# Conv-sequence block on one Trainium2 core: softmax laid out by key with no maximum where the weights bound the scores, groups emitted as a pipeline of five steps, one pool of PSUM banks

## The chip, the cores and the metric

The kernel runs on one core of one Trainium2 chip. The core's engines work side by side, each in its own queue's order: TensorE (PE, matrix products into the eight banks of PSUM), VectorE (DVE), ScalarE (ACT, functions such as the exponential), GpSimd (POOL), and SyncE (SP), which issues most DMA transfers. The metric is the device time of one execution in microseconds (us).

## The reference

Input x is [2, 256, 128, 128]: batch, time, band, channel. Three residual steps: attention over time (causal, 4 heads of 32 channels, one sequence of 256 steps for each batch and band), attention over bands (128 bands of one time step, only pairs at most 16 apart), and a feed-forward of 512 with gelu. Each begins with a layer norm over the channels. All data is float32.

```python
def _mha(x, wi, bi, wo, bo, h, mask):
    qkv = x @ wi.T + bi
    ...
    scores = jnp.einsum('...hqd,...hkd->...hqk', q, k) * (1.0 / np.sqrt(dh)) + mask
    attn = jax.nn.softmax(scores, axis=-1)
    o = jnp.einsum('...hqk,...hkd->...hqd', attn, v)
    ...
    return o @ wo.T + bo
...
xt = _ln(x, ln_t_w, ln_t_b).transpose(0, 2, 1, 3)
x = x + _mha(xt, t_wi, t_bi, t_wo, t_bo, H_T, cm).transpose(0, 2, 1, 3)
xf = _ln(x, ln_f_w, ln_f_b)
x = x + _mha(xf, f_wi, f_bi, f_wo, f_bo, H_F, bm)
xn = _ln(x, ln_n_w, ln_n_b)
h = jax.nn.gelu(xn @ w1.T + b1, approximate=False)
x = x + (h @ w2.T + b2)
```

The weight matrices are drawn with a standard deviation of 0.02; the norms' weights are ones, all biases zeros.

## The kernel before

Work goes in groups of four token tiles of 128 rows (NT = 4). In the first stage a group is two sequences of 256 steps; eight bands (four groups) are loaded at once by two DMAs (L278), and the result of each group is stored to a scratch tensor in memory (L287). There are 128 such groups. In the second stage a block is 16 time steps (L299): four groups of attention over bands, then the same four groups through the feed-forward, then the store (L332). There are 32 blocks.

Every group is written from start to end before the next, by `norm_transposed` (L113) and `attention` (L134). In order: statistics of the rows (L118, L119 on DVE), their inverse deviation (rstd, L121 and L122 on POOL), the normalized rows (xh, L126 on DVE), transposes on PE (L129) and a scaled copy by ACT (xnT, L131); the products for queries, keys and values (L144, L148, L153) with copies by ACT and DVE. The scores stand with queries on the partitions and keys along the row. For each pair of heads a score tile of two banks is filled by a product of the identity with a bfloat16 mask (L166), to which the scores are added (L173, 32 rows of the array for each head). DVE takes the negated maximum of each row (nmax, L181 for bands, L187 for time), ACT the exponential with that shift, 128 or 256 columns at a time, and each row's sum through its accumulator (p and rsum, L195), DVE the reciprocal (L203), POOL the division (L206 for bands, L214 for time). p is then transposed on PE block by block (tp, L221) and copied to SBUF by DVE and ACT in turn (pT, L226, L228). The weighed values (op, L239) come out transposed, are copied with the value bias (oT, L245), multiplied by the output weights (yp, L248), and added to the rows (L249).

A scheduler of the framework orders the instructions of each engine; it follows the order in which the program wrote them, and moves forward what its model finds ready. Score tiles have their own pool of two tiles with two banks each, and every other PSUM tile shares a pool of four banks (L57, L58). Exponentials and gelus need different function tables on ACT; `order_act` (L255) makes them take turns by the block.

## Time and profile before

| | us |
|---|---|
| median of three runs | 6695.87 (6692.37 to 6696.81) |
| span of the profiled execution | 6687.7 |
| PE busy | 4965.1 |
| ACT busy | 3223.4 |
| DVE busy | 2769.3 |
| POOL busy | 2263.4 |

The runs were timed without the profiler, the span comes from the profiled execution, from its first to its last instruction. "Busy" is the time in which at least one instruction of the engine was under way; PE's products are pipelined and overlap. One float32 product appears as two records of PE, the two passes over its moving operand; its weight loads are listed apart as PEld. In a group's row the shapes stand as partitions x elements, then the count, the total and the mean of one in ns, and after the bar the idle time of the engine just ahead and what ended it. A row of the timeline has start, length, engine, line, operation, tiles, shape and the count of records that were merged.

### The profile page before, as it was taken

To read this page: it belongs to the slowest core of one execution; us is meant where nothing else is said; L and a number is where in the kernel's file an instruction comes from. 1 tells how busy PE (TensorE), PEld (TensorE's weight loads), DVE (VectorE), ACT (ScalarE), POOL (GpSimd) and SP (SyncE) were. 2 spreads that over 40 slices of the span, in tenths; PEclk is the share of its full clock that TensorE was granted. 3 is DMA by queue.
4 is the path that set the end of the run, shared out by engine and by line. 5 is a ranking of instruction groups with operands and counts; after the bars stand their busy time and mean duration, and the time that the engine had idled before them with its cause. 6 is when DMAs were issued, how large, how long until landed. Compare 5 with 4: busy or idle time off the path is not lost. (4 is left out here: it accounts for less than half of the span.)

```text
span 6687.7 us, 95401 instructions
## 1 busy us (share of the span) xinstructions
PE 4965.1 (74%) x34688; PEld 3392.3 (51%) x34816; DVE 2769.3 (41%) x8068; ACT 3223.4 (48%) x10688; POOL 2263.4 (34%) x2348
## 2 busy tenths in 40 slices
PE   6777777777777777777777777777676767677767
PEld 4444454444444444454555555555454545455555
DVE  4444444444444444434344444444344444444433
ACT  4444444444444444444454444444444444454544
POOL 4333333333333333433232323233333333233332
PEclk8878787778787877788888888888888888888888
DMA  1000000000000000000000000000000000000000
GB/s 48 20 24 25 23 20 24 24 23 20 24 24 23 20 24 23 24 20 20 24 15 24 14 26 14 26 13 26 13 26 13 26 13 26 13 26 13 20 7 13
DMA packets 222968, 141.61 MB, mean 21 GB/s; under 512 B 7968, under 2 KB 205984, under 8 KB 222496
## 3 DMA queue, kind: packets, MB, share of 16 engines
q1 hardware_dynamic: 221248, 134.45, 7.1%
q8 instruction: 274, 4.49, 0.3%
q14 instruction: 198, 1.62, 0.1%
q10 hardware_dynamic: 1248, 1.05, 0.1%
HBM read 68.36 MB, written 67.11 MB: 20 GB/s over the span
## 5 line engine op out<-in xcount | busy, mean ns | idle before, releaser
L195 ACT ACTIVATE p<-sp,nmax 128x128 f32<-128x128 f32 (+1 forms) x4096 | 1547.6, 414 | 870.0 <-DVE nmax L187 553.6
L221 PE MATMUL tp<-ident,p 128*128 128x128 f32 x5120 | 1207.6, 401 | 275.6 <-POOL p L206 228.0
L221 PEld LDWEIGHTS tp<-ident,p 128*128 128x128 f32 x5120 | 930.1, 209 | 743.0 <-POOL p L206 394.6
L214 POOL TENSOR_TENSOR p<-p,rsum 128x256 f32<-128x256 f32 (+1 forms) x1024 | 823.9, 826 | 952.2 <-DVE rsum L203 820.9
L206 POOL TENSOR_TENSOR p<-p,rsum 128x1024 f32<-128x1024 f32 x256 | 485.2, 1895 | 1493.5 <-DVE rsum L203 1493.5
L195 ACT ACTIVATION_READ_ACCUMULATOR p<-sp,nmax 128x1 f32 x4096 | 929.0, 227 | 0.0
L228 ACT COPY pT<-tp 128x384 f32<-128x384 f32 (+1 forms) x768 | 395.1, 518 | 945.8 <-PE tp L221 942.5
L226 DVE COPY pT<-tp 128x384 f32<-128x384 f32 (+1 forms) x768 | 453.8, 598 | 698.9 <-PE tp L221 689.3
L173 PE MATMUL sp<-kT,qT 32*128 32x128 f32 (+1 forms) x8192 | 740.7, 362 | 0.0
L166 PEld LDWEIGHTS <-ident_b 128*128 128x128 bf16 x1536 | 193.8, 128 | 1007.0 <-issue 663.8
L166 PE MATMUL sp<-mask_t,ident_b 128*128 128x384 bf16 x1024 | 383.1, 472 | 384.6 <-ACT p L195 381.7
L203 DVE RECIPROCAL rsum<-rsum 128x4 f32<-128x4 f32 (+1 forms) x768 | 141.9, 185 | 1221.9 <-ACT p L195 1204.0
L239 PE MATMUL op<-pT,v 128*32 128x128 f32 (+1 forms) x8192 | 526.6, 319 | 86.6 <-DVE pT L226 55.0
L166 PE MATMUL sp<-mask_f,ident_b 128*128 128x512 bf16 x384 | 204.3, 601 | 517.0 <-ACT p L195 517.0
L173 PEld LDWEIGHTS sp<-kT,qT 32*128 32x128 f32 x8192 | 490.8, 214 | 172.9 <-issue 142.1
L317 ACT ACTIVATE hT<-hp,cols_sb 128x512 f32<-128x512 f32 x512 | 351.8, 687 | 392.3 <-PE hp L316 389.5
L187 DVE TENSOR_REDUCE nmax<-sp 128x2 f32<-128x256 f32 (+1 forms) x1024 | 505.0, 545 | 56.6 <-PE sp L173 56.5
L131 ACT ACTIVATE xnT<-xp,cols_sb 128x512 f32<-128x512 f32 x384 | 298.4, 777 | 475.0 <-PE xp L129 475.0
L327 PEld LDWEIGHTS zp<-w2T_sb,hT 128*128 128x128 f32 x4096 | 487.5, 192 | 61.5 <-issue 58.4
L316 PE MATMUL hp<-xnT,w1T_sb 128*128 128x512 f32 x1024 | 471.9, 599 | 42.8 <-ACT xnT L131 27.8
L327 PE MATMUL zp<-w2T_sb,hT 128*128 128x128 f32 x4096 | 499.0, 275 | 0.1
L121 POOL TENSOR_SCALAR rstd<-mv 128x4 f32<-128x4 f32 x384 | 91.8, 242 | 1190.5 <-DVE mv L119 1190.5
(55 smaller groups left out, 5974.5 us busy)
## 6 DMA issues: line engine op xcount, KB each, us to landing
xt<-in_x SPq DMA_DIRECT2D x64, 512.0 KB, 5.5
x<-rd SPq DMA_DIRECT2D x256, 128.0 KB, 1.9
out<-res SPq DMA_DIRECT2D x128, 256.0 KB, 2.3
xb<-x SPq DMA_DIRECT2D x32, 0.5 KB, 6.2
w1T_sb<-in_w1T ACTq DMA_DIRECT2D x1, 256.0 KB, 5.4
w2T_sb<-in_w2T ACTq DMA_DIRECT2D x1, 256.0 KB, 7.1
t_wiT_sb<-in_t_wiT ACTq DMA_DIRECT2D x1, 192.0 KB, 2.5
f_wiT_sb<-in_f_wiT ACTq DMA_DIRECT2D x1, 192.0 KB, 4.5
```

What stands on the lines that cost most here:

```text
L166: nc.tensor.matmul(sp[:, j, 0 : nb * P], ident_b, mask.rearrange("p a b -> p (a b)"), start=True, stop=False,)
L173: nc.tensor.matmul(sp[:, j, n * P : (n + len(ks)) * P], qT[r, qi * P : (qi + 1) * P], kT[r, ks[0] * P : (ks[-1] + 1) * P], start=False, st ...
L187: nc.vector.tensor_reduce(nmax[:, :, ri : ri + 1], sp[:, :, n * P : (n + len(ks)) * P], AX.X, ALU.max, negate=True,)
L195: e = nc.scalar.activation(p[:, j, n * P : (n + len(ks)) * P], sp[:, j, n * P : (n + len(ks)) * P], AF.Exp, bias=nmax[:, j, ri : ri + 1], ...
L206: nc.gpsimd.tensor_tensor(pv, pv, rsum.rearrange("p j n -> p (j n)").unsqueeze(2).to_broadcast([P, 2 * nb, P]), ALU.mult,)
L214: nc.gpsimd.tensor_tensor(pv, pv, rsum[:, :, ri : ri + 1].to_broadcast([P, 2, len(ks) * P]), ALU.mult,)
L221: nc.tensor.transpose(tp[:, n * P : (n + 1) * P], p[:, j, n * P : (n + 1) * P], ident)
L226: nc.vector.tensor_copy(t, tp[:, 0 : nb * P])
L228: nc.scalar.copy(t, tp[:, 0 : nb * P])
L239: nc.tensor.matmul(op[r, qi * P : (qi + m) * P], v[:, ki, r], pT[bi, h][:, n * P : (n + m) * P], start=first, stop=last,)
L316: nc.tensor.matmul(hp_, w1T_sb[:, j * P : (j + 1) * P], xnT, start=True, stop=True)
L327: nc.tensor.matmul(zp[:, i], hT[:, j, i * P : (i + 1) * P], w2T_sb[:, j, :], start=(j == 0), stop=(j == NI - 1),)
```

## The change

The program now begins with `fold` (L334), which multiplies the norms' weights and the score scale into the projection weights, turns the norms' biases into the query bias, the output rows and the feed-forward's bias, and computes a test: with the Gram matrices of a head's query and key weights, the sum of their elementwise product is compared with a bound, and the value and output weights are compared with another. The result goes to a register of every engine, and a branch takes one of two paths: `shifted_path` is the former kernel in full, `bounded_path` the new one.

In `bounded_path` the scores are laid out with keys on the partitions and queries along the row: K is the stationary and Q the moving operand. There is no mask product, no maximum, no transpose of p. ACT takes the exponential of a whole head at once (384 columns over time, 512 over bands), and POOL then sets the masked weights to zero by affine selects, two for each sequence (four heads, 512 elements each) or two for each pair of heads over bands (1024 elements each). The weighed values are a product with p itself (op); a second product, of ones with p, gives each query's sum on all 32 channels of the head (rp). ACT computes Exp(−Ln(rp)), DVE one step of Newton's method on it and the product with op (`divide`: t, u, oT), with the sign turned around in the negated output weights wn. The copies of xnT and of the keys are now DVE's.

A group is an object with steps, and `run` writes the steps of neighbouring groups in turn: in round n stand the transposes of group n + 1, the division of n − 1, the first half of the scores of n, queries and keys of n + 1, the second half of n, the normalizing of n + 2, the output of n − 1, the values of n + 1, the statistics of n + 3, and the weighing of n; loads are written five groups ahead. All PSUM tiles take one bank each from a pool of eight. The table for Exp and Ln is loaded once by name where attention follows a feed-forward.

```diff
-    ps_s = ctx.enter_context(tc.tile_pool(name="ps_s", bufs=2, space=PSUM))
-    ps = ctx.enter_context(tc.tile_pool(name="ps", bufs=4, space=PSUM))
+        self.ps = ctx.enter_context(tc.tile_pool(name="ps", bufs=8, space=PSUM))
...
+def fold(tc, k):
...
+            wf = const.tile([P, 3 * C], F32, name=f"wf{a}")
+            nc.vector.tensor_scalar(wf[:, 0:C], wi[:, 0:C], col(c0), scale, ALU.mult, ALU.mult)
+            nc.vector.tensor_scalar(wf[:, C : 3 * C], wi[:, C : 3 * C], col(c0), None, ALU.mult)
...
+            nc.tensor.matmul(gq, wf[:, 0:C], wf[:, 0:C], start=True, stop=False)
...
+            nc.tensor.matmul(gk, wf[:, C : 2 * C], wf[:, C : 2 * C], start=True, stop=True)
...
+            nc.vector.tensor_tensor(gs, gk, gs, ALU.mult)
...
+                nc.vector.tensor_reduce(tests[r, 3 * a : 3 * a + 1], gs[r, r], AX.X, ALU.add)
...
+                ok[:, 3 * a : 3 * a + 1], tp[:, 3 * a : 3 * a + 1], SAFE * SAFE / (C * (C + 1)), None, ALU.is_le
...
+    return nc.values_load(flag[0:1, 0:1], min_val=0, max_val=1)
...
+    def invert(self):
...
+        path.exp_set(nc.scalar.activation(ln, self.rp, AF.Ln))
...
+        path.exp_set(nc.scalar.activation(self.r0, ln, AF.Exp, scale=-1.0))
...
+    def divide(self):
...
+        nc.vector.tensor_tensor(t, self.rp, self.r0, ALU.mult)
...
+        nc.vector.tensor_tensor(u, self.op, self.r0, ALU.mult)
...
+        nc.vector.scalar_tensor_tensor(self.oT, t, 2.0, u, ALU.subtract, ALU.mult)
...
+class OverTime(Attention):
...
+        for h in range(H):
+            r = rows_of(h)
+            sp = path.bank([P, W], "sp")
+            nc.tensor.matmul(
+                sp[:, 0 : 2 * P], self.kT[r, a : a + P], self.qT[r, a : a + 2 * P], start=True, stop=True
+            )
+            nc.tensor.matmul(
+                sp[:, 2 * P : W], self.kT[r, a + P : a + 2 * P], self.qT[r, a + P : a + 2 * P],
+                start=True, stop=True,
+            )
+            path.exp_set(nc.scalar.activation(self.p[:, s, h, :], sp, AF.Exp))
+        for n in (0, 2):
+            blk = self.p[:, s, :, n * P : (n + 1) * P]
+            nc.gpsimd.affine_select(
+                out=blk, in_=blk, compare_op=ALU.is_ge, fill=0.0, base=0,
+                pattern=[[0, H], [1, P]], channel_multiplier=-1,
+            )
...
+class OverBands(Attention):
...
+        for s in (1, -1):
+            nc.gpsimd.affine_select(
+                out=blk, in_=blk, compare_op=ALU.is_ge, fill=0.0, base=BAND,
+                pattern=[[0, len(heads)], [0, NT], [-s, P]], channel_multiplier=s,
+            )
...
+        for n in range(-5, len(groups) + 1):
...
+            do(n + 5, "load")
+            do(n + 1, "transpose", "bias")
+            do(n - 1, "divide")
+            do(n, "first_half")
+            do(n + 1, "queries_keys")
+            do(n, "second_half")
+            do(n + 2, "normalize")
+            do(n - 1, "output")
+            do(n + 1, "values")
+            do(n + 3, "statistics")
+            do(n, "weigh")
...
+    bounded = fold(tc, k)
+    with tc.If(bounded > 0) as cmp:
+        bounded_path(tc, k, x, out)
+    with cmp.Else():
+        shifted_path(tc, k, x, out)
```

What stands in PE's queue in the middle of the first stage, before the change, from the weighing of one group to the scores of the next (the number behind a tile's name counts tiles, so that tiles of one group lie close together):

```order
L239 MATMUL op_3972<-pT_3970,v_3846 32x128
L248 MATMUL yp_3991<-t_woT_sb_85,oT_3989 128x128 x4
L129 MATMUL xp_4018<-ident_93,xh_4017 128x128 x4
L144 MATMUL qp_4029<-xnT_4027,t_wiT_sb_81 128x512
L148 MATMUL kp_4033<-xnT_4027,t_wiT_sb_81 128x512
L153 MATMUL vp_4037<-t_wiT_sb_81,xnT_4027 128x128 x4
L173 MATMUL sp_4044<-kT_4035,qT_4031 128x128 x2
L173 MATMUL sp_4044<-kT_4035,qT_4031 128x256 x2
```

And PE's queue in the first stage of the changed program, from the last scores of one round to the first scores of the next:

```order
L582 MATMUL sp_3438<-qT_3297,kT_3301 128x128
L550 MATMUL yp_3449<-wn0_106,oT_3397 128x128 x4
L524 MATMUL vp_3457<-wf0_103,xnT_3389 128x128 x4
L608 MATMUL op_3477<-pt_3399,v_3339 32x256 x4
L613 MATMUL op_3477<-pt_3399,v_3339 32x128 x4
L608 MATMUL op_3477<-pt_3399,v_3339 32x256 x4
L620 MATMUL rp_3494<-pt_3399,ones_87 32x512 x4
L613 MATMUL op_3477<-pt_3399,v_3339 32x128 x4
L622 MATMUL rp_3494<-pt_3399,ones_87 32x2x128 x4
L467 MATMUL xp_3507<-ident_76,xh_3444 128x128 x4
L579 MATMUL sp_3523<-qT_3420,kT_3424 128x256
L582 MATMUL sp_3523<-qT_3420,kT_3424 128x128
```

The output of one group, the values of a second and the transposes of a third now stand between the scores and the weighing of a fourth and the next scores; a head's two score products stand side by side, where two heads used to alternate (x2).

DVE's queue in the first stage before, where the statistics of a new load stand:

```order
L249 TENSOR_TENSOR rd<-yp,rd 128x512
L126 TENSOR_SCALAR xh<-xt,mv,rstd 128x128 x4
L119 BN_AGGR mv<-stats 128x2 x4
L157 COPY v<-vp 128x512
L187 TENSOR_REDUCE nmax<-sp 128x2 x4
L118 BN_STATS stats<-xt 128x6 x8
L203 RECIPROCAL rsum<-rsum 128x4
L118 BN_STATS stats<-xt 128x6 x8
```

DVE's queue in the changed program at such a place, once in four groups:

```order
L457 TENSOR_SCALAR xh<-xt,mv,rstd 128x128 x4
L540 TENSOR_TENSOR t<-rp,r_4867 128x512
L542 TENSOR_TENSOR u<-op,r_4867 128x512
L448 BN_AGGR mv<-stats 128x2 x4
L446 BN_STATS stats<-xt 128x6 x8
L544 SCALAR_TENSOR_TENSOR oT<-t,u 128x512
L446 BN_STATS stats<-xt 128x6 x8
L517 COPY kT<-kp 128x512
```

The statistics of four groups, sixteen instructions, stand ahead of and behind the oT that the output product reads; they used to stand among the maxima and reciprocals.

PE's queue in the attention over bands of the changed program, one round:

```order
L642 MATMUL sp_27112<-qT_27020,kT_27024 128x128 x4
L642 MATMUL sp_27118<-qT_27020,kT_27024 128x128 x4
L510 MATMUL qp_27126<-xnT_27102,wf1_143 128x512
L515 MATMUL kp_27130<-xnT_27102,wf1_143 128x512
L667 MATMUL op_27071<-pf_27003,v_26948 32x128 x14
L670 MATMUL rp_27088<-pf_27003,ones_87 32x512 x2
L642 MATMUL sp_27134<-qT_27020,kT_27024 128x128 x4
L642 MATMUL sp_27140<-qT_27020,kT_27024 128x128 x4
```

Here the scheduler put most of the weighing of a group (op, the fifth row, which reads the selected pf of heads 2 and 3 among others) behind the next group's first scores and the queries and keys of the one after; in other rounds it stands ahead of them.

More of the change, by code (lines that the diff above doesn't have):

```diff
@@ L11 @@
 BF16 = mybir.dt.bfloat16
+I32 = mybir.dt.int32
 AF = mybir.ActivationFunctionType
@@ new lines, with bias, hidden, first_half @@
+class FeedForward(Group):
+    def bias(self):
+        path = self.path
+        self.res = path.work.tile([P, NT, P], F32, name="res")
+        path.nc.gpsimd.tensor_tensor(
+            self.res, self.src(), path.k.rows[:, 2:3, :].to_broadcast([P, NT, P]), ALU.add
+        )
+    def hidden(self, js):
+        path, nc = self.path, self.path.nc
+        for j in js:
+            hp = path.bank([P, NT * P], "hp")
+            nc.tensor.matmul(hp, path.k.w1f[:, j * P : (j + 1) * P], self.xnT, start=True, stop=True)
+            path.gelu_set(
+                nc.scalar.activation(
+                    self.hT[:, j, :], hp, AF.Gelu, bias=path.k.b1[:, j : j + 1], scale=1.0
+                )
+            )
+    def first_half(self):
+        self.hT = self.path.work.tile([P, self.path.k.NI, NT * P], F32, name="hT", bufs=2)
+        self.hidden((0, 1))
+    def second_half(self):
+        self.hidden((2, 3))
+    def output(self):
+        path, nc = self.path, self.path.nc
+        NI = path.k.NI
+        zp = path.bank([P, NT, P], "zp")
+        for i in range(NT):
+            for j in range(NI):
+                nc.tensor.matmul(
+                    zp[:, i], self.hT[:, j, i * P : (i + 1) * P], path.k.w2T[:, j, :],
+                    start=(j == 0), stop=(j == NI - 1),
+                )
+        nc.vector.tensor_tensor(self.res, zp, self.res, ALU.add)
+        self.store(self.res)
@@ L29, in conv_seq_kernel, with bounded_path @@
+def bounded_path(tc, k, x, out):
+    with ExitStack() as ctx:
+        BoundedPath(ctx, tc, k).run(x, out)
 @with_exitstack
```

840 lines of the change are left out of this document (589 added, 251 removed).

## The prediction

> **What bounds the kernel now.** I read the engines' shares on the page first, then equal stretches of the two stages, then the chain that ended last, then single groups by shape.
>
> ```profile
> span 6687.7 us, 95401 instructions
> PE 4965.1 (74%) x34688; PEld 3392.3 (51%) x34816; DVE 2769.3 (41%) x8068; ACT 3223.4 (48%) x10688; POOL 2263.4 (34%) x2348
> ...
> 21.60:2844.00 2822.40, 2180.09 (x14160) 1392.00 (x14160) 1200.61 (x3578) 1335.32 (x4720) 1063.83 (x1306) 0.80 0.08 23
> 2890.00:6650.00 3760.00, 2714.27 (x20096) 1951.71 (x20222) 1531.47 (x4344) 1848.04 (x5865) 1166.71 (x992) 0.87 0.07 19
> ...
> 6546.00:6570.00 24.00, 24.00 (x143) 17.78 (x143) 6.11 (x16) 10.58 (x15) 3.08 (x4) 1.00 0.11 33
> 6576.00:6640.00 64.00, 38.32 (x321) 27.50 (x323) 23.30 (x61) 32.08 (x133) 19.01 (x16) 0.82 0.00 1
> ```
>
> No engine is full. In the last two rows (columns: stretch, its length, busy us of PE, PEld, DVE, ACT, POOL, granted clock, DMA) the feed-forward has PE busy all 24 us at clock 1.00; attention over bands has it busy 38 of 64 us at 0.82, and each other engine half or less. The DMA share is under a tenth. So the feed-forward is bound by PE, attention by something that no engine's sum shows. The chain shows it (start, us, what):
>
> ```profile
> 6482.31 1.24 DVE nmax L181
> 6483.63 1.08 ACT p L195 x6
> 6484.93 1.62 ACT p L195 x9
> 6486.91 1.90 POOL p L206
> 6488.86 1.97 PE tp L221 x8
> ...
> 6493.55 0.59 ACT pT L228
> 6494.19 1.07 PE op L239 x26
> 6495.29 0.70 ACT oT L245
> 6496.03 1.16 PE yp L248 x8
> ...
> 6502.51 1.24 DVE nmax L181
> ...
> 6546.89 3.44 PE hp L316 x8
> 6551.21 3.13 PE zp L327 x28
> 6554.33 3.44 PE hp L316 x8
> ```
>
> One group of bands, maximum to maximum, takes 6502.51 − 6482.31 = 20.20 us, and its own steps fill it in single file: maximum, exponentials, division, transposes, weighing, output. **Attention is bound by the latency of one group**, since groups stand one behind another in every queue. A feed-forward group takes 6554.33 − 6546.89 = 7.44 us, PE alone. Over time the first and the last group's query product stand at
>
> ```profile
> 21.61 2.07 PE L144 MATMUL qp<-xnT,t_wiT_sb 128*128 128x512 f32 x2 [0.87 <-ACT xnT L131]
> 2844.02 1.12 PE L144 MATMUL qp<-xnT,t_wiT_sb 128*128 128x512 f32 x2 [0.87 <-ACT xnT L131]
> ```
>
> so 127 periods take 2822.4 us, 22.2 each. From 2866 to the end 32 blocks (four groups of bands, four feed-forwards) take 3822 us, 119.4 each: 4 × 20.2 + 4 × 7.44 = 110.6, and 9 at the changes.
>
> **The change part by part.** The durations it needs:
>
> ```profile
> 1507.89 0.95 PE L173 MATMUL sp<-kT,qT 32*128 32x128 f32 x16
> 1520.83 1.27 PE L239 MATMUL op<-pT,v 128*32 128x256 f32 x20
> 6593.35 1.72 PE L173 MATMUL sp<-kT,qT 32*128 32x128 f32 x32
> ...
> L317 ACT ACTIVATE hT<-hp,cols_sb 128x512 f32<-128x512 f32 x512 | 351.8, 687 | 392.3 <-PE hp L316 389.5
> L228 ACT COPY pT<-tp 128x384 f32<-128x384 f32 x512 | 245.4, 484 | 477.6 <-PE tp L221 474.3 <-PE op L239 1.7
> L317 ACT ACT_TABLE_LOAD x32 | 41.1, 1283 | 0.6
> L214 POOL TENSOR_TENSOR p<-p,rsum 128x512 f32<-128x512 f32 x512 | 531.9, 1039 | 0.0
> L206 POOL TENSOR_TENSOR p<-p,rsum 128x1024 f32<-128x1024 f32 x256 | 485.2, 1895 | 1493.5 <-DVE rsum L203 1493.5
> L97 POOL TENSOR_SCALAR_AFFINE_SELECT mask_f<-mask_f 128x512 bf16<-128x512 bf16 x2 | 1.3, 634 | 0.1
> L90 POOL TENSOR_SCALAR_AFFINE_SELECT mask_t<-mask_t 128x128 bf16<-128x128 bf16 x2 | 0.5, 292 | 0.0
> L282 POOL TENSOR_TENSOR rd<-xt,rows_sb 128x512 f32<-128x512 f32 x128 | 162.2, 1268 | 45.1 <-DMA x<-rd 36.5 <-DMA xt<-in_x 8.5
> L122 POOL TENSOR_TENSOR rstd<-rstd,mhalf 128x4 f32<-128x4 f32 x384 | 399.7, 1047 | 26.1
> L126 DVE TENSOR_SCALAR xh<-xb,mv,rstd 128x128 f32<-128x128 f32 x512 | 271.4, 593 | 297.4 <-PE xp L129 225.2 <-issue 64.8 <-POOL res L321 7.4
> L126 DVE TENSOR_SCALAR xh<-xt,mv,rstd 128x128 f32<-128x128 f32 x512 | 141.5, 339 | 0.0
> L118 DVE BATCH_NORM_STATS2 stats<-xt 128x6 f32<-128x128 f32 x512 | 105.8, 278 | 70.6 <-DMA xt<-in_x 70.2
> L249 DVE TENSOR_TENSOR rd<-yp,rd 128x512 f32<-128x512 f32 x128 | 88.5, 691 | 391.9 <-PE yp L248 391.9
> ```
>
> *Removed*, all on the chain: mask products, maxima (DVE), reciprocals, the division on POOL, transposes of p with their copies. *Added*: selects that zero masked weights (POOL), sums by a product with ones (rp), Ln and Exp on ACT for 1/sum, three DVE passes (t, u, oT). Copies of xnT and kT go from ACT to DVE, folded weights replace their scales.
>
> *PE work of a group* (records are passes, two to a product). Queries and keys: the chain's 3.44 us for eight passes of 512 columns gives 1.72. Values and output: 3.13/28 a pass, eight passes, 0.89 each. Transposes: 0.5. Scores over time: the first row is one sequence's four heads, 0.95 when heads alternate; now a head's two products stand together. Strictly one after another a head holds its 32 rows for (2 × 256 + 2 × 128) columns at 0.43 per 512: 0.55 after the previous head, 2.3 for four. In file, even with alternating heads, each product holds off the next by its first pass: 4 × 0.11 + 4 × 0.22 = 1.3 for the first row's sequence, and 16 × 0.11 + 0.27 of drain = 2.0 for the third row's bands. The rows are 0.95 and 1.72: products on other rows overtake. I take 1.2, nearer the row than to 2.3. So 2.4 for two sequences. Weighing: 1.27 for 20 passes, 32 make 1.6 with one drain. Sums: 2 × (512 + 256) columns with four heads side by side, 1.3 to 1.5. Sum over time: 0.5 + 1.72 + 2 × 0.89 + 2.4 + 1.6 + 1.5 = **9.5 us**. Bands: scores 2.2 (bounds 1.7 and 3.2), weighing 1.3, sums 1.3: **8.8 us**. Feed-forward: unchanged, 7.44.
>
> The Trainium skill ("TensorE: Matmul & The Clock Gate", Part 3: Packing small matmuls — row/col tiling) says that products are strict FIFO in start and end. By that rule the scores of two sequences cost 4.6 instead of 2.4; the 0.95 row does not agree, but it shows alternating heads, not heads in a row, so the rule is rival B.
>
> *The wait that ends last now, over time.* Let 0 be the end of a group's sums. ACT: Ln and Exp, 0.69 each and a hand-over, 1.6, and behind them in its queue stands all that follows of the next group; four exponentials of 384 columns at 0.49, 3.6; query copy, 4.2; four more, 6.3. POOL then selects twice. A select costs 0.178 + 0.00089 per column (292 and 634 ns rows): 0.63 for 512, and 1.04 if it ran like the L214 row; so 7.7 to 8.5. DVE: xnT to 1.5, four xh 2.6, t and u 4.0, aggregates 4.4, oT 5.1. PE: transposes 0.5, scores 1.7, wait for xnT, queries and keys 3.6, scores 4.8, wait for oT 5.2, output and values 7.0, weighing and sums 10.1. The selects end under that. So **PE with its two short waits sets the period**. DVE and POOL can block each other: xh took 339 ns alone and 593 on average where L301 ran beside it; oT meets the first selects, up to 0.6, so 10.1 to 10.7, I take 10.4. One group in four has eight statistics (0.22 apart) ahead of oT: 1.8/4 = 0.45. Period **10.8 us**, where 22.2 was.
>
> *Bands.* The selects are 1024 columns, 1.09 each (1.9 if like L206), two after the last exponential, and weighing needs them: Ln, Exp 1.7; two exponentials of 512 (0.69 each, 0.6 apart, an estimate between the 484 and 687 rows) 3.0; query copy 3.6; scores of heads 2 and 3 at 4.8; exponentials 6.1; selects with hand-overs 8.6; the rest of weighing and sums 10.4. PE waits near 1.5 us of it. **10.5 us**, where 20.2 was. POOL's sum, 4 × 1.09 + 1.27 + 1.29, is 6.9, and DVE's 7 × 0.69 (xnT, kT, v, t, u, oT, output) + 1.1 + 0.9 + 0.4 = 7.2: neither binds.
>
> *Feed-forward and changes.* 7.44 stays. At a change PE goes on with the neighbour's products; I leave 3 us a block for table loads (1.28 each, two) and for the run of 16 statistics before the second feed-forward, where 9 stood. Block: 4 × 10.5 + 4 × 7.44 + 3 = 74.8.
>
> *Queues.* SP now holds each load five groups ahead, behind stores:
>
> ```profile
> xt<-in_x SPq DMA_DIRECT2D x64, 512.0 KB, 5.5
> xb<-x SPq DMA_DIRECT2D x32, 0.5 KB, 6.2
> ```
>
> Landing in 5.5 and 6.2 us lies under five groups of ten: nothing. POOL's additions (1.27) stand ahead of the selects, under the exponentials; ahead of a block's first select four of them stand, under the feed-forward, or 5 us a block if they came late.
>
> *Bank pool.* Eight banks instead of 4 + 2 × 2 cost nothing: each one's earlier reader has ended on the count above; a missed one shows as PE waiting on ACT.
>
> *Start.* fold adds some 45 DVE instructions in a chain with small products, a flag read by all engines, and only then are the first inputs loaded; three groups fill the pipeline. The first query product stood at 21.6; I take 60, bounds 35 and 110. The branch itself is in no row: 0 to some us.
>
> *Clock.* It was 0.80 to 0.82 where PE had gaps and 1.00 where it had none; with gaps of 0.5 to 1.5 us I count 1.0.
>
> Sum: 128 × 10.8 + 32 × 74.8 + 60 = 1382 + 2394 + 60 = 3836. The runs' median of 6695.87 lies 8 above the profile's span; with it **3845 us**.
>
> **Rivals.**
> - A, all waits hidden, PE alone: 128 × 9.5 + 32 × (4 × 8.8 + 29.8) + 60 = 3356, with the 8, 3365. For it: the feed-forward shows PE dense. Against: the bands' loop of 10.4.
> - B, heads in single file: 2.2 more over time, 1.0 more in the bands' loop: 128 × 3.2 = 410, 4255. For it, the order (a head's products together); against, the 0.95 and 1.72 rows.
> - C, selects at the price of L206 and L214: bands' loop +1.6, over time +0.5: 128 × 2.1 = 269, 4115. For it, both work on float32 p in place; against, the rows of selects themselves.
> - D, the clock stays at 0.8: over time PE work 9.5/0.8 = 11.9 swallows the waits, 12.4 with the statistics, +1.6; bands' PE share of the loop, 2.9 us, +0.7: 128 × 2.3 = 294, 4140. For it, row-group products fill a quarter of the array; against, gaps too short.
> - E, slower than before: the test fails and the shifted path runs, the kernel of before with 35 us of fold in front: 6731. It decides at 30²/(128 × 129) = 0.0545 for the sum, over heads, of the products of the query and key Gram matrices. With weights of deviation 0.02, the query's divided by √32, the diagonals give 128 × 0.0016 × 0.0512 = 0.0105. Five times under.
>
> **How the numbers follow.** Forecast 0.48, A 0.11, B 0.17, C 0.12, D 0.10, E 0.02. The prediction is 3845; the forecast's own range is 3600 to 4050. Reaching over B, C and D with some of them together, and to just above A: 3420 to 4400. A measurement can tell 0.2% from no change; only E is not faster: 0.975 faster, 0.005 within, 0.02 slower.
>
> **What would show it.** Period of the query product over time near 10.8, with PE busy over 85% and clock above 0.95 (D: 0.8). Last record of a sequence's scores 1.2 us after the first (B: 2.3). Select rows of 634 and 1090 ns (C: 1040 and 1900). In bands, PE's longest wait on POOL selects, a block near 75 us. Table loads still 64. First query product near 45. The prediction is wrong if DVE or POOL, blocking each other, exceed 10 us a group, or if bank waits tie groups together again.

## The result and the profile after

The changed kernel takes 4108.43 us (median of four runs, 4102.52 to 4109.43); the kernel before, timed beside it, 6696.34. The ratio is 0.6134, interval 0.6125 to 0.6143. The profiled execution has a span of 4106.3 us and took 4108.16, so 2 us lie around it. A later run of the kernel before shows the same (6693.05 with a span of 6691.3); so the 8 us that the prediction added seem to be mostly a difference between executions. The head of the page:

```profile
span 4106.3 us, 77158 instructions
PE 3682.2 (90%) x31270; PEld 2508.3 (61%) x31270; DVE 2327.0 (57%) x6702; ACT 1595.4 (39%) x2880; POOL 1909.9 (47%) x2182
```

Three stretches of the trace (length, busy us of PE, PEld, DVE, ACT and POOL, granted clock, DMA share), from the first to the 128th query product over time, the 30 blocks from the second on, and a short one that is spoken of below:

```profile
36.53:1412.44 1375.91, 1224.49 (x13129) 802.36 (x13129) 848.98 (x2375) 640.40 (x1387) 672.89 (x888) 0.94 0.18 50
1503.19:4006.41 2503.22, 2276.90 (x16802) 1580.81 (x16801) 1367.04 (x3963) 886.86 (x1381) 1152.13 (x1197) 0.96 0.09 25
836.00:844.50 8.50, 7.48 (x64) 5.33 (x64) 4.50 (x13) 0.00 (x0) 1.70 (x2) 0.60 0.12 33
```

A group over time takes 1375.91/127 = **10.83 us** (predicted 10.8), a block 2503.22/30 = **83.4** (predicted 74.8). Times 32, the block is 276 us too long, a little more than the 263 by which the time was missed; the start, earlier than forecast, gives some back. In the first two stretches PE is idle for a tenth and its clock is under 1, so neither is dense.

*Over time.* The 10.83 is no common period: three of four groups take 9.25 us, every fourth 14 to 17. PE's timeline over one short and one long group:

```profile
821.30 1.13 PE L510 MATMUL qp<-xnT,wf 128*128 128x512 f32 x2
...
830.55 1.12 PE L510 MATMUL qp<-xnT,wf 128*128 128x512 f32 x2
...
832.46 0.73 PE L579 MATMUL sp<-qT,kT 32*128 32x256 f32 x8
833.00 0.42 PE L582 MATMUL sp<-qT,kT 32*128 32x128 f32 x8
837.02 2.08 PE L550 MATMUL yp<-wn,oT 128*128 128x128 f32 x8 [3.60 <-DVE oT L544]
838.89 1.92 PE L524 MATMUL vp<-wf,xnT 128*128 128x128 f32 x8
...
846.09 1.13 PE L510 MATMUL qp<-xnT,wf 128*128 128x512 f32 x2
```

830.55 − 821.30 = 9.25, with PE dense; 846.09 − 830.55 = 15.54. Of the 6.3 more, 3.60 is the wait for oT, and the rest half clock behind it: yp takes 2.08 us, which takes 1.16 at full clock (at 2117.88); over the stretch from 836 to 844.5 the granted clock is 0.60. What oT waited for, in the timelines of DVE, SP and POOL:

```profile
832.00 0.68 DVE L542 TENSOR_TENSOR u<-op,r 128x512 f32<-128x512 f32 x1
832.60 0.37 DVE L448 BATCH_NORM_AGGREGATE mv<-stats 128x2 f32<-128x6 f32 x4
834.47 1.65 DVE L446 BATCH_NORM_STATS2 stats<-xt 128x6 f32<-128x128 f32 x8 [1.50 <-DMA xt<-in_x]
836.03 0.94 DVE L544 SCALAR_TENSOR_TENSOR oT<-t,u 128x512 f32<-128x512 f32 x1
...
830.14 1.00 SPq L766 DMA_DIRECT2D xt<-in_x  x2
...
828.85 1.27 POOL L498 TENSOR_TENSOR rd<-xt,orow 128x512 f32<-128x512 f32 x1 [1.50 <-DMA x<-rd]
```

t and u were done at 832.7, yet oT stands behind eight statistics of the load, and the load was issued at 830.14, when POOL's addition (828.85 + 1.27) had read the oldest input buffer for the last time. The addition had itself waited for a store. Nothing needed these statistics yet: counted in DVE's records, statistics run 12 to 14 groups ahead of the next group to be divided, where the program's order has 3.

*Over bands.* PE's and then ACT's and DVE's timeline of one block:

```profile
2126.09 1.03 PE L670 MATMUL rp<-pf,ones 128*32 128x512 f32 x4
2127.05 1.71 PE L642 MATMUL sp<-qT,kT 32*128 32x128 f32 x16
2131.25 2.05 PE L550 MATMUL yp<-wn,oT 128*128 128x128 f32 x8 [2.49 <-DVE oT L544]
...
2140.11 2.27 PE L642 MATMUL sp<-qT,kT 32*128 32x128 f32 x28
2144.37 2.04 PE L550 MATMUL yp<-wn,oT 128*128 128x128 f32 x8 [1.99 <-DVE oT L544]
...
2154.41 1.03 PE L670 MATMUL rp<-pf,ones 128*32 128x512 f32 x4
2158.94 1.13 PE L550 MATMUL yp<-wn,oT 128*128 128x128 f32 x8 [3.50 <-DVE oT L544]
...
2127.17 0.60 ACT L532 ACTIVATE ln<-rp 128x512 f32<-128x512 f32 x1 [2.04 <-PE rp L670]
2127.80 0.63 ACT L534 ACTIVATE r<-ln 128x512 f32<-128x512 f32 x1
2128.46 0.69 DVE L540 TENSOR_TENSOR t<-rp,r 128x512 f32<-128x512 f32 x1 [1.47 <-ACT r L534]
2129.07 0.68 DVE L542 TENSOR_TENSOR u<-op,r 128x512 f32<-128x512 f32 x1
2129.79 1.32 DVE L544 SCALAR_TENSOR_TENSOR oT<-t,u 128x512 f32<-128x512 f32 x1
```

From the end of the sums (2127.12) to the output product it is 4.1 us of Ln, Exp, t, u, oT (4.2 and 3.5 at the two later places); what stood between them in PE's queue was 1.7 or 2.3 us of scores, or nothing. Three such waits make 8 us in this block, 7 on average. PE waited 201 us for oT and 17 for selects in the stretch from 1600 to 4000, where the prediction had the selects as its longest wait:

```profile
PE yp L550 <- DVE oT L544: 201.1, 87, 3.5
PE op L667 <- POOL pf L648: 17.0, 19, 0.9
```

(Columns: who waited for whom, us in total, times, longest.) The groups by shape, with the mean of one in ns:

```profile
L648 POOL TENSOR_SCALAR_AFFINE_SELECT pf<-pf 128x1024 f32<-128x1024 f32 x512 | 595.8, 1167 | 889.8 <-ACT pf L644 875.7
L589 POOL TENSOR_SCALAR_AFFINE_SELECT pt<-pt 128x512 f32<-128x512 f32 x512 | 350.8, 705 | 301.4 <-ACT pt L586 301.2
```

Selects of 1167 and 705 ns stand against 1090 and 634 predicted. The first query product starts at 36.5, where 45 was named and 60 counted with the filling of the pipeline.

### The profile page after: what moved, and what is told of

It is laid out like the page before. It is cut to its first block, busy times and chain, and to the rows that moved or that the text cites. A ratio compares the mean times of both kernels' runs of the same rounds, so it can differ in the third digit from the quotient of the medians.

```text
span 4106.3 us, 77158 instructions
## 1 busy us (share of the span) xinstructions
PE 3682.2 (90%) x31270; PEld 2508.3 (61%) x31270; DVE 2327.0 (57%) x6702; ACT 1595.4 (39%) x2880; POOL 1909.9 (47%) x2182
## 4 chain that ended last, share of the span: by engine, by line
PE 56%; DVE 5%; ACT 3%; POOL 1%; issue 1%; ACTq 0%; POOLq 0%; DVEq 0%
PE zp L709 11%; PE hp L689 11%; PE sp L642 7%; PE rp L670 6%; PE op L667 4%; PE xp L467 4%; PE yp L550 4%; PE vp L524 3%; PE qp L510 3%; PE kp L515 3%; DVE oT L544 2%; DVE t L540 1%; POOL pf L648 1%; DVE u L542 1%; ACT r L534 1%; ACT ln L532 1%
## 5 line engine op out<-in xcount | busy, mean ns | idle before, releaser
L648 POOL TENSOR_SCALAR_AFFINE_SELECT pf<-pf 128x1024 f32<-128x1024 f32 x512 | 595.8, 1167 | 889.8 <-ACT pf L644 875.7
L550 PE MATMUL yp<-wn,oT 128*128 128x128 f32 x2048 | 333.1, 312 | 357.4 <-DVE oT L544 357.4
L691 ACT ACTIVATE hT<-hp,b 128x512 f32<-128x512 f32 x512 | 341.4, 687 | 386.0 <-PE hp L689 382.0
L589 POOL TENSOR_SCALAR_AFFINE_SELECT pt<-pt 128x512 f32<-128x512 f32 x512 | 350.8, 705 | 301.4 <-ACT pt L586 301.2
L689 PE MATMUL hp<-xnT,w1f 128*128 128x512 f32 x1024 | 485.3, 605 | 0.0
L586 ACT ACTIVATE pt<-sp 128x384 f32<-128x384 f32 x1024 | 420.1, 495 | 127.2 <-PE sp L582 126.8
L642 PEld LDWEIGHTS sp<-qT,kT 32*128 32x128 f32 x4096 | 375.3, 186 | 107.6 <-issue 43.9
L642 PE MATMUL sp<-qT,kT 32*128 32x128 f32 x4096 | 420.4, 283 | 0.0
L451 POOL TENSOR_TENSOR rstd<-rstd,mhalf 128x4 f32<-128x4 f32 x384 | 403.8, 1057 | 23.6
L524 PE MATMUL vp<-wf,xnT 128*128 128x128 f32 x2048 | 312.9, 304 | 0.0
```

Source lines behind the costliest of these rows:

```text
L451: nc.gpsimd.tensor_tensor(self.rstd, self.rstd, path.k.mhalf, ALU.pow)
L524: nc.tensor.matmul(vp[:, i], self.xnT[:, i * P : (i + 1) * P], wv, start=True, stop=True)
L550: nc.tensor.matmul(yp[:, i], self.oT[:, i * P : (i + 1) * P], path.k.wn[self.which], start=True, stop=True)
L586: path.exp_set(nc.scalar.activation(self.p[:, s, h, :], sp, AF.Exp))
L589: nc.gpsimd.affine_select(out=blk, in_=blk, compare_op=ALU.is_ge, fill=0.0, base=0, pattern=[[0, H], [1, P]], channel_multiplier=-1,)
L642: nc.tensor.matmul(sp[:, c], self.kT[r, c], self.qT[r, c], start=True, stop=True)
```

## The experiments

Twelve kernels, in the order in which they ran. Each table row gives the time, then, from the starts of the query products, the mean period over time (first to 128th, by 127) and the mean block (second to 32nd, by 30).

| kernel | us | period | block |
|---|---|---|---|
| the change | 4108.43 | 10.83 | 83.4 |
| e1_four_x_buffers | 4026.57 | 10.37 | 82.8 |
| e1b_four_statistics_buffers | 4032.88 | 10.45 | 82.8 |
| e2b_weigh_before_scores | 4009.72 | 10.85 | 80.4 |
| e5_two_bank_pools | 4088.96 | 11.49 | 80.3 |
| e1c_statistics_held | 3951.94 | 9.75 | 83.2 |
| e4_one_select_of_two | 3991.51 | 10.75 | 80.1 |
| e6_no_pipeline | 6064.17 | 18.41 | 114.4 |
| c2_longer_pipeline | 4394.88 | 15.15 | 75.1 |
| c3_order_by_stage | 3807.98 | 10.56 | 75.1 |
| c4_heads_alternate_in_bands | 3818.63 | 10.51 | 75.6 |
| c5_bias_held | 3622.68 | 9.07 | 75.1 |
| c6_bias_held_heads_alternate | 3662.71 | 9.07 | 76.6 |

c2 to c6 were timed in rounds (medians of four); the others are single runs (the four of the change lie within 7 us).

**e1: a fourth input buffer.**

```diff
-        self.xpool = ctx.enter_context(tc.tile_pool(name="xpool", bufs=3))
+        self.xpool = ctx.enter_context(tc.tile_pool(name="xpool", bufs=4))
```

> One more input buffer (4 instead of 3). In the changed kernel three of four groups over time take 9.25 us from query product to query product and every fourth 14 to 17. Theory (a late load stands in front of oT): the next load can be issued only when POOL has read the oldest buffer's last group, DVE's queue holds the eight statistics of that load ahead of oT, so DVE waits for the DMA and PE for oT, and then runs at half clock. With a buffer more the load lands a group or more earlier: all four periods 9.2 to 9.6 us, first to 128th query product near 1190 us instead of 1376, granted clock in the stage near 1.0, total near 3925 (3900 to 3960). Rival (the statistics' own time on DVE, 16 times 0.22 us in one group, is what delays oT): only the wait for the DMA itself goes, 1.5 us in 32 places, 4060. Second rival (the load isn't on the path): 4108.

82 us came, 59 of them over time, where some 180 were expected. Most long groups still took 11 to 16 us, and DVE's timeline (of one at 1124) shows the same picture as before, with a smaller wait:

```profile
1127.75 0.49 DVE L446 BATCH_NORM_STATS2 stats<-xt 128x6 f32<-128x128 f32 x2 [1.55 <-DMA xt<-in_x]
1128.15 0.67 DVE L544 SCALAR_TENSOR_TENSOR oT<-t,u 128x512 f32<-128x512 f32 x1
```

The buffer let the load go earlier, and the scheduler, which puts forward what its model finds ready, moved the statistics forward by as much: in DVE's records they are now 16 groups ahead of the division, where they were 12 to 14. My theory of a buffer too few falls; that the statistics' place matters stays open, and the rival of 4060 is not far off either.

**e1b: fewer buffers for the statistics**, so that they can't run as far ahead.

```diff
-        self.small = ctx.enter_context(tc.tile_pool(name="small", bufs=6))
+        self.small = ctx.enter_context(tc.tile_pool(name="small", bufs=4))
```

> Three input buffers as in the changed kernel, but four buffers instead of six for the statistics, so that the scheduler can't place statistics as many groups ahead. Theory (a late load in front of oT, by their places in DVE's queue): the load lands as late as before, but the statistics that wait for it stand later in DVE's queue, behind oT; the long period goes as with a fourth input buffer, first to 128th query product near 1200 us, total 3920 to 3970. Rival (the load's lateness holds the pipeline back wherever the statistics stand): no change, 4108; between the two, some of it.

About as e1, between the two. The statistics are 12 groups ahead at every group. A count of buffers only shifts how far the scheduler runs ahead; it does not set the place.

**e2b: weighing ahead of the next scores, over bands.** An order alone, with no wait, is put between the last sum of a group and the next group's first scores (and the second half of the feed-forward's first group).

```diff
+                path.behind(mm, path.last.get("rp"))
...
+        path.last["rp"] = mm.ins
```

> In the stage over bands the weighing of a group is held ahead of the next group's first scores in PE's queue, as the program writes it; the scheduler had put it behind them in two rounds of four. Theory (order: with the weighing late, PE has only 1.7 to 2.3 us of scores left to do while Ln, Exp, t, u and oT take 3.7): PE's waits for oT of 2.5, 2.0 and 3.5 us in a block shrink to under 1, 1 and 2, part of it comes back as waits of op for the selects (near 1.5 us in a round), block 76 to 79 us instead of 83.6, total 3870 to 3960. Rival (the selects' latency sets the round): what op waits for POOL takes the place of all that yp waited for DVE, block 82 to 84, total 4060 to 4130. The stage over time does not change by either.

A block falls by 3.0 us to 80.4, less than the 5 to 8 expected; over time nothing changes. PE's waits, from 1600 to 4000:

```profile
PE yp L550 <- DVE oT L544: 89.2, 60, 1.6
PE qp L510 <- DVE xnT L469: 57.4, 28, 2.3
PE op L668 <- POOL pf L649: 30.7, 60, 0.5
```

The wait for oT fell from 201 to 89, as the theory has it, and the selects did not take its place (30.7 for 17.0, longest 0.5): the rival falls. A wait for xnT came in instead, 2 us a block. The granted clock in the blocks rose from 0.96 to 0.99, and PE's busy time per block fell by 1.5 us, half of the gain.

**e5: two pools of banks.**

```diff
-        self.ps = ctx.enter_context(tc.tile_pool(name="ps", bufs=8, space=PSUM))
+        self.ps = ctx.enter_context(tc.tile_pool(name="ps", bufs=4, space=PSUM))
+        self.ps_s = ctx.enter_context(tc.tile_pool(name="ps_s", bufs=4, space=PSUM))
```

> The eight banks split into two pools of four, one for score tiles, one for all others, as the kernel before had it in its way. Prediction's step (each bank's earlier reader has ended, so the pool itself costs and brings nothing): 4090 to 4130, periods as in the changed kernel. Rival (one pool is what lets the steps of neighbouring groups stand side by side: op and rp hold two of the four banks until u is done, and xp, qp, kp, vp, yp take turns in the other two): PE waits for ACT and DVE at qp, kp and xp, period over time 11.5 to 13 and block 90 to 95, total 4400 to 4700.

The time, 4089, lies just under the prediction's window, but for no good reason: over time it lost 83 us, over bands it gained some 100. PE's timeline over time shows the loss:

```profile
805.50 0.72 PE L579 MATMUL sp<-qT,kT 32*128 32x256 f32 x6
...
806.80 1.16 PE L550 MATMUL yp<-wn,oT 128*128 128x128 f32 x8 [0.37 <-DVE oT L544]
...
809.24 0.40 PE L613 MATMUL op<-pt,v 128*32 128x128 f32 x8
809.57 0.71 PE L579 MATMUL sp<-qT,kT 32*128 32x256 f32 x4
```

With four banks for scores, eight tiles of a group go through them in turn; the scores come in pieces (x6, and x4 behind another group's products, where all eight passes stood together), so fewer heads run side by side. A short group takes 10.2 to 10.4 instead of 9.25, and PE's busy time over time grows by 103 us. That the pieces come from the pool of four is read from this timeline, not tested by itself. Over bands the scheduler's order came out another way too; what part of that gain is the pool's own was not separated.

**e1c: statistics held where the program writes them**, behind the oT of their round, over time only.

```diff
-            nc.vector.bn_stats(stats[:, i, :], self.src()[:, i, :])
+            st = nc.vector.bn_stats(stats[:, i, :], self.src()[:, i, :])
+            if isinstance(self, OverTime):
+                path.behind(st, path.last.get("oT"))
```

> In the stage over time each group's statistics are held in DVE's queue behind the oT of the round in which the program writes them, buffers as in the changed kernel. With a fourth input buffer, and with four statistics buffers, the long period only fell from 15.4 to 13 us, since the scheduler again put statistics right behind the load and DVE still waited for the DMA ahead of oT. Theory (what stands ahead of oT in DVE's queue makes the long period: the wait for the load and eight statistics): with four statistics behind each oT, and none ahead of it on a late load, all periods are 9.25 to 9.5 us, first to 128th query product 1180 to 1215 us instead of 1376, granted clock 1.0, total 3920 to 3950. Rival (the bias addition and the load hold one group in four back wherever the statistics stand: POOL's addition waits for stores): every fourth period still 13 or more, total 4030 to 4108. The stage over bands stays at 83.6 a block by either.

Nearly a hit (first to 128th product 1238 us, 23 over the window): the period falls to 9.75, the time by 156 us, the block stays at 83.2. The long groups are gone (median period 9.30, 120 of 127 under 10.6), with the same three input buffers; the statistics are now 3 groups ahead in DVE's records. So what stood ahead of oT in DVE's queue made them. The stretch over time, first to 128th query product:

```profile
32.85:1270.61 1237.76, 1177.79 (x13128) 740.18 (x13128) 980.32 (x2418) 640.16 (x1387) 679.89 (x893) 0.99 0.20 55
```

PE's clock rose from 0.94 to 0.99, and its busy time fell by 47 us without a product less.

**e4: one select of two.**

```diff
-        for n in (0, 2):
+        for n in (0,):
...
-        for s in (1, -1):
+        for s in (1,):
```

> Leaves out the second of the two selects in both stages: over time the masked weights of each sequence's second diagonal square stay, over bands those on one side of the band. Theory (order and clock; selects lie beside PE's work): POOL is busy 256 times 0.71 and 256 times 1.17 us less, some 480, and the time hardly follows: over time 9.25 in three of four periods as before, block 82 to 84, total 4060 to 4110. Rival (the selects' latency ends the wait of op in the bands, rival C of the prediction): a band round gets 1.2 us shorter, block 77 to 79, total 3900 to 3960.

Between the two. Over time nothing to speak of (10.75): POOL lies beside PE there. A block lost 3.3 us. This can't be read as the selects' price: the scheduler placed the weighing otherwise, in most rounds ahead of queries and keys, as e2b does by hand; e2b has nearly the same block (80.4) with all selects. PE's direct waits for selects over bands were 17 us in the change.

**e6: no pipeline.**

```diff
-            do(n + 1, "transpose", "bias")
-            do(n - 1, "divide")
-            do(n, "first_half")
...
+            do(n, "statistics", "normalize", "transpose", "bias", "queries_keys", "values")
+            do(n, "first_half", "second_half", "weigh", "divide", "output")
```

> The softmax by key, the folded weights and the one bank pool stay; each group's steps are written from start to end before the next group's, and only loads stay five groups ahead. Theory (the pipeline brings most: in single file a group over time takes xp 0.6, xnT 0.9, queries and keys 1.9, values 0.9, scores 2.4, the rest of the exponentials 1.8, a select and a half 1.3, weighing and sums 3.2, Ln to oT 3.7, output 0.95, so 17.6, and PE's gaps bring the clock down): period over time 17 to 20, block 4 times 17 to 20 and 4 times 7.4 to 10, total 5400 to 6100. Rival (less work is what brings it, and the scheduler lays neighbouring groups side by side by itself): period under 13, total 4200 to 4700.

Hit: 6064, the period 18.4 (17.1 in most groups). Without the order the rest of the change (softmax by key, folded weights, one pool, early loads) brings 632 us of the 2588; the order of emission brings the other 1956, the higher clock among them. The clock is 0.85 and 0.81 in the two stages, where the kernel before had 0.80 and 0.87.

**c2: a longer pipeline.** A round is now, in its core:

```diff
+            do(n, "first_half")
+            do(n + 1, "transpose")
+            do(n - 2, "output")
+            do(n + 2, "statistics")
+            do(n + 1, "queries_keys")
+            do(n - 1, "weigh")
+            do(n, "second_half")
+            do(n + 2, "normalize")
+            do(n + 1, "values")
+            do(n - 1, "divide")
```

> A candidate from the theories: weighing of group n-1 stands behind the queries and keys of n+1, output of n-2 behind the first scores of n, so PE has some 5 us of other work between the sums and the output, and 5 us between the last scores and the weighing; statistics held behind oT as in e1c; four input buffers, more buffers for rows and hidden layer. If order on PE and DVE is all that keeps PE from being dense, period over time 9.2 to 9.4 and block 66 to 71 us: 128 times 9.3 and 32 times 66 to 71 and 60, total 3360 to 3530. Rival (something else comes up when PE is dense: DVE and POOL blocking each other, or banks): period 10 or more, block 75 or more, total 3740 and up.

Slower than the change in sum (ratio to the kernel before 0.6563, 0.6552 to 0.6574), out of two opposite effects, and by its numbers the rival's case. The block fell to 75.1, with the clock at 1.00; place of the weighing, output, statistics and buffers changed together, so the 8.3 us are not split among them. Over time a group took 15.2. DVE's timeline there, then PE's:

```profile
810.58 0.86 DVE L446 BATCH_NORM_STATS2 stats<-xt 128x6 f32<-128x128 f32 x4
...
813.80 1.25 DVE L458 TENSOR_SCALAR xh<-xt,mv,rstd 128x128 f32<-128x128 f32 x2 [1.48 <-POOL rstd L452]
814.97 0.68 DVE L470 COPY xnT<-xp 128x512 f32<-128x512 f32 x1
...
815.79 2.05 PE L511 MATMUL qp<-xnT,wf 128*128 128x512 f32 x2 [3.92 <-DVE xnT L470]
```

Statistics, rstd and xh of one group now fall in one round, and xnT, for which PE waits 3.9 us at half the clock, stands behind that chain in DVE's queue. So PE was not dense there, and the rival's reason, DVE and POOL blocking each other or banks, is not what the rows show.

**c3: each stage its own round.** Over time the rounds of the change with statistics held; over bands and feed-forward those of c2.

```diff
+            if not time(n - 2):
+                do(n - 2, "output")
...
+            if time(n - 1):
+                do(n - 1, "output")
```

> The longer pipeline for bands and feed-forward alone; over time the rounds of the changed kernel with the statistics held behind oT. The longer pipeline took 74.9 us a block over bands, but 15.2 a group over time, where it computed the statistics of n+2 in the round that normalizes n+2, so that the copy xnT stood behind that chain in DVE's queue. If that is the reason and the two stages don't act on each other: first to 128th query product 1190 to 1245 us, block 74 to 76, total 3700 to 3760. Rival (the held statistics or the larger buffers themselves slow the stage over time): 1900 there again, total 4390.

The block is 75.1 as foreseen; over time the period is 10.56, so neither theory holds. Three groups of four take 9.0 to 9.8, every fourth mostly 14 to 16 again, with the statistics in their place. POOL's timeline of one, then PE's:

```profile
517.45 1.26 POOL L499 TENSOR_TENSOR rd<-xt,orow 128x512 f32<-128x512 f32 x1 [7.35 <-DMA x<-rd]
518.66 1.23 POOL L591 TENSOR_SCALAR_AFFINE_SELECT pt<-pt 128x512 f32<-128x512 f32 x2
...
519.35 0.64 PE L610 MATMUL op<-pt,v 128*32 128x256 f32 x8 [1.40 <-POOL pt L591]
...
521.88 0.83 PE L610 MATMUL op<-pt,v 128*32 128x256 f32 x8 [1.51 <-POOL pt L591]
```

The six buffers that c2 brought for rd had let the scheduler put POOL's addition four groups ahead of the selects instead of two, as POOL's records count. There it waits for the store that frees its buffer, the store stands behind a load, and selects wait behind the addition.

**c4: two heads in turn.**

```diff
-                nc.tensor.matmul(sp[:, c], self.kT[r, c], self.qT[r, c], start=True, stop=True)
+        for i in range(NT):
+            for h, sp in zip(heads, sps):
+                r, c = rows_of(h), slice(i * P, (i + 1) * P)
+                nc.tensor.matmul(sp[:, c], self.kT[r, c], self.qT[r, c], start=True, stop=True)
```

> As c3, and over bands the scores of two heads are written tile by tile in turn, so that neighbouring products lie on different rows of the array, where a head's four products stood in a row. In the records a head's eight passes start 0.11 us apart and the second head's first only when the first's sixth has started, while over time, with two products a head, four heads run side by side. Theory (a product can start ahead of products before it on other rows, but only ahead of a few): now the two heads run side by side throughout, 16 passes in 1.0 us instead of 1.7, 0.6 to 0.7 less in each of 8 places of a block, total 150 to 180 us below c3. Rival (128-column passes are bound by something that heads share, such as loading the weights): no difference.

The mechanism is right, the gain nothing (0.5702, 0.5692 to 0.5711, against 0.5685, 0.5676 to 0.5695, of c3). PE's timeline of c3 from scores to output:

```profile
2554.96 1.71 PE L644 MATMUL sp<-qT,kT 32*128 32x128 f32 x16
2556.60 0.66 PE L468 MATMUL xp<-ident,xh 128*128 128x128 f32 x4
2557.09 1.06 PE L552 MATMUL yp<-wn,oT 128*128 128x128 f32 x8
```

and of c4 at such a place:

```profile
2552.72 1.16 PE L643 MATMUL sp<-qT,kT 32*128 32x128 f32 x16
...
2555.92 1.13 PE L552 MATMUL yp<-wn,oT 128*128 128x128 f32 x8 [1.46 <-DVE oT L545]
```

16 passes take 1.16 us instead of 1.71; but the chain to oT is as long as ever, so PE waits, and the clock in the blocks falls from 1.00 to 0.97.

**c5: the addition held as well.**

```diff
+        self.path.behind(add, self.path.last.get("select"))
```

> As c3, with POOL's bias addition held behind the selects of the round in which the program writes it. In c3 three of four groups over time took 9.0 us, but every fourth still 14 to 16: the six buffers for rd had let the scheduler put the addition four groups ahead in POOL's queue, where it waited for the store that freed its buffer, itself behind a load, with selects and rstd queued behind it. Theory (it is what stands in front in POOL's queue): all periods 9.0 to 9.6, first to 128th query product 1145 to 1215 us instead of 1341, total 3610 to 3680. Rival (the store's delay behind the load holds something else back too, so the long period stays): 3780 to 3810. The stage over bands stays at 75 a block.

Hit: 3622.68 us, ratio 0.5412 (0.5403 to 0.5421), the fastest. The addition is one group ahead of the selects in POOL's records. The period is 9.07, 125 of 127 groups under 9.5; PE is dense over time at clock 1.00:

```profile
30.72:1182.11 1151.39, 1146.33 (x13129) 741.63 (x13129) 1022.61 (x2390) 640.04 (x1387) 636.54 (x881) 1.00 0.22 59
1279.63:3533.34 2253.71, 2143.13 (x16803) 1532.27 (x16801) 1327.69 (x3960) 869.76 (x1380) 1157.79 (x1196) 1.00 0.10 28
```

**c6: c5 with two heads in turn, and queries and keys ahead of the output.**

```diff
+            if band:
+                do(n + 1, "queries_keys")
             if not time(n - 2):
                 do(n - 2, "output")
```

> As c5, with the scores of two heads over bands in turn as in c4, and the queries and keys of the next group ahead of the output product. In c4 two heads' scores fell from 1.64 to 1.09 us, yet the block did not get shorter, since with PE's work shorter PE waited for oT (0.3 to 1.5 us) and went on at half clock. Theory (2 us more of work between the sums and the output cover oT): block 71 to 73.5 us instead of 75, total 80 to 130 below c5. Rival (feed-forward rounds and the wait for xh set the block): block 74.5 to 76, total as c5.

Missed: the block is 76.6, 1.4 above c5 (ratio 0.5473, 0.5464 to 0.5483). PE's wait for oT did not go:

```profile
PE yp L553 <- DVE oT L546: 44.2, 50, 1.5
```

In c5 it is 9.1 us in the same stretch (1600 to 3500), in c4 89.3 from 1600 to 3700. Waits for gelu (36 us) and xnT (24) came beside it, and the clock in the blocks is 0.97. Which one to mend next was not tried.

## Why the prediction was right, and where it was not

**Direction and size.** PE did take over as the bound, busy 90%, and 2588 us were gained where 2851 were forecast. e6 shows that the gain is mostly that of the order. The "two short waits" of each group did not come: three groups of four have next to none, and the fourth has a long one. (One reading was off without effect: the DMA share is 0.11 in the feed-forward's row, not "under a tenth".)

**Period over time: right by luck, by errors that cancel.** The count was 9.5 of PE's work, 0.9 of waits and 0.45 of statistics. PE's work at full clock is 1146.33/127 = 9.03 (c5); the scores are a part of the difference: 1.2 us a half was taken, and the rows at 832.46 and 833.00 end 0.96 after the first start. The waits of a short group are 9.25 − 9.03 = 0.2. Against these two, the term "1.8/4 = 0.45" was mis-sized: the count had eight statistics ahead of oT, 1.8 us, but not that they would wait there for their load, nor the clock after it. The long groups cost 10.83 − 9.25 = 1.6 us a group, and 9.03 + 0.2 + 1.6 is the 10.83 again. The step that failed is that of the queues, "under five groups of ten: nothing": loads are written five groups ahead, but buffer and scheduler decide when they are issued and where their readers stand.

**The block: 83.4 for 74.8.** It splits by the stretches of the change and of c5, whose clock is 1.00. PE's work is 2143.13/30 = 71.4 a block, where the prediction counted 4 × 8.8 + 29.8 = 65.0. The rest of the change's busy time, 2276.90/30 − 71.4 = 4.5, I put down to its slower clock, though the orders differ too. Idle time is (2503.22 − 2276.90)/30 = 7.5, where 9.8 were allowed (4 × 1.7 + 3). So the idle time was not under-counted in sum; two terms failed. "Scores 2.2" a group of bands are 2 × 1.64 = 3.3 (from the start of the scores to that of the transposes in the c3 rows), 4.3 us a block of the 6.4 that PE's work was short; the other 2.1 are a net of smaller terms that were not traced. And the clock, "I count 1.0", was 0.96.

**What ended the wait.** "In bands, PE's longest wait on POOL selects" was the wrong one: by the rows above, oT was waited for twelve times as long. The step that failed is the bands' loop: it has no term from Exp over t, u and oT to the output product, and it is counted on the order as written, while the scheduler had moved the weighing behind scores, queries and keys, as one listing in the section on the change shows. e2b settles that this order costs 3.0 us a block; c2, c3 and c5, with output a round later among other things, are 8.3 below the change.

**Bank pool.** "Cost nothing" holds over time, and there one pool even brings 0.65 us a group (e5). Over bands it is open: with two pools the block was 3.1 us shorter, under another order.

**The rivals.** A (all waits hidden) is what c5 comes near over time. B, heads in single file: over time the records refute it, and with them the rule of the Trainium skill ("TensorE: Matmul & The Clock Gate", Part 3: Packing small matmuls — row/col tiling) that products start and end strictly in program order. The program writes 256, 128 columns for each head in turn, and PE's queue has them so, yet all eight passes of 256 columns start ahead of those of 128. Over bands, with four products of a head in a row, B's price did come: scores of 3.3 a group, where the prediction's upper bound was 3.2, and c4 shows 1.71 against 1.16. C (selects at the price of the divisions) is refuted by the selects' own rows, 1167 and 705 ns against C's 1900 and 1040. What the selects cost over bands, e4 can't separate. D (clock) came in part, 0.94 and 0.96, not 0.8. E did not come; the flag let the new path run.

## What to carry to other kernels

In a pipeline written by hand and ordered by a scheduler, look at what stands **ahead** of the instruction that the bottleneck waits for, in its own engine's queue: work that runs ahead as far as its buffers allow ends up there, waiting for a transfer. More buffers move that wait, they don't remove it; an order that holds such work at its place does (156 us by the statistics, 185 by the addition). Shortening the bound engine's work brought nothing (c4) where it only covered another engine's chain. Moving the consumer of that chain a round away came with the shorter block of c2 and c3; 2 us more of work ahead of it (c6) was not enough.

## What the runs showed of the hardware

- Products on other rows of the array can start ahead of products before them in PE's queue, but here only so far: two products a head (four passes) let four heads run side by side (0.96 us for 16 passes), four products a head do not (1.71 us for two heads; 1.16 in turn).
- A wait of PE of 2 to 4 us can halve its clock, but its length does not decide it: after waits of 1.99 and 2.49 us (yp at 2144.37 and 2131.25) yp took 2.04 and 2.05, after one of 3.50 (at 2158.94) 1.13. In the trace's record of the granted clock every change lies on a fixed grid of 3.41 us: half clock from 2129.95 to 2136.78 and from 2143.61 to 2150.44, none behind the wait of 3.50, across which the point 2157.26 lies. Over the whole run PE's busy share in the 3.41 us before a point goes with it: at full clock, no fall came after a share over 0.71, and one after every share under 0.40. Between them, as in these three, something else decides, which was not tested. The Trainium skill ("TensorE: Matmul & The Clock Gate", Part 1: The HAM clock gate) has the clock fall after an idle window of about 3.4 us; waits of 2 us were enough here.
- Ln, Exp and three passes of DVE take 3.5 to 4.2 us from the sums to the output product (three places of one block), and over bands that chain, not the selects of POOL, is what PE waited for.
